# Diagonal chunk pairs computed on and above the diagonal only, the rest filled by TensorE transposes

## The chip, the cores and the metric

The kernel runs on one core of one Trainium2 chip. The metric is device time in microseconds (us) of that core. Before the change three runs took 1889.49, 1889.62 and 1890.78 us (median 1889.62); the profiled execution has a span of 1888.3 us and a mean granted TensorE clock of 0.987.

## The reference

```python
# layer 0, for each of 4 images; q is 4096 blocks-of-channel rows by 128 values here
energy = jnp.einsum('bci,bcj->bij', q, q)
d = jnp.sqrt(jnp.diagonal(energy, axis1=1, axis2=2))
energy = energy / (d[:, :, None] * d[:, None, :])
attn = jax.nn.softmax(energy, axis=-1)
out = jnp.einsum('bcj,bij->bci', q, attn)
out = gamma * out + xs
# layer 1, written short here; the reference spells it out; tokens of 128 channels
t = t + linear_attention(layernorm(t))      # 8 heads, no softmax
t = t + moe(layernorm(t))                   # router over 8 experts, top 2
```

The attention of layer 0 has 4096 positions with a vector of 128 values each. All vectors have length one once the energy is divided by `d`, so the scores are symmetric and at most 1, and no maximum is needed: `exp(energy)` is a symmetric 4096 by 4096 matrix, and its row sums divide the output at the end.

## The kernel before, in words

Everything is float32. For each image `b` (4 of them), `prep` loads four pieces `xx` of x, transposes them on TensorE to `qT` (positions on partitions), squares and reduces on VectorE (`sq`, `ss`), takes the inverse root on GpSimd (`rn`, line 109), scales (`qs`, line 190), and transposes back on TensorE (`ptn`, line 193) to `qn` (values on partitions, length one), which ScalarE copies out. A piece gives two chunks of 512 positions; there are 8 chunks (`NCH`) of 4 blocks (`NJ`) of 128.

`attend` walks over the pairs of chunks `(i, jc)` with `jc <= i`. A pair has four steps. In a step TensorE makes 128 by 512 scores (`pe`, line 242), ScalarE takes the exponential into `pr` with row sums (line 244), and TensorE multiplies by the values into the output bank `po` of chunk `i` (line 233), one step later than its scores. For `jc < i` the symmetric partner is needed too: VectorE transposes `pr` in 32 by 32 squares into `F` (line 248), 16 DMAs move the squares to their places in `G` (line 260, issued by SyncE), and later four matmuls of `G` (line 207, `transposed_share`) give chunk `jc` its part from chunk `i`, while ScalarE sums `G` (line 212) and VectorE adds the bank `pg` to the output `o` (line 218). Of `po` and `pg` there is one bank each, of `pe`, `pt` (all transposes and small products) and `py` two each. The pair on the diagonal, `jc == i`, is its own partner: its four steps compute all 512 by 512 scores, both halves of the symmetric square. It comes last in each `i`.

The transposed shares wait in the list `late`; one of their four steps is recorded in each step of `attend`, from `LAG` steps after the pair ended.

Layer 1 of image `b-1` (`layer1`, from line 273) is a generator of 151 small steps. While `attend(b)` runs, the main loop advances it, and the `prep` of image `b+1`, at set rates: a stream `(generator, begin, end, count)` takes `count` steps evenly between the steps `begin` and `end` of the 144. Layer 1 first divides the outputs by the row sums (`pbd`, `df`, line 342), adds them to the tokens on GpSimd (`T`, line 350), takes row statistics on VectorE (`bs_a` to `dm_a`, lines 311 to 320), the inverse root on GpSimd (`rsa`, line 109), `nba` on VectorE (line 322), normalises on ScalarE (`xn`, line 325) and forms the Gram matrix on TensorE (`pgram`, line 368). After that come attention rows, router and experts (`py`, lines 525 and 532). Layer 1 of the last image runs alone at the end.

The recording layer does not keep the written order as it stands: it plans each engine's order ahead of the run from the dependences, the buffers and estimates of its own, and the built program has one fixed list of instructions per engine. The engines meet at semaphores. The lists of the profiled execution are those of the built program, and they can be read for both kernels.

Of the kernel before, what the change touches and what calls it, by code (L numbers as in the profile page):

```python
# [1 line left out]

# [7 lines left out]
F32 = mybir.dt.float32  # L10
BF16 = mybir.dt.bfloat16
AF = mybir.ActivationFunctionType
# [6 lines left out]
def kernel(  # L19
# [10 lines left out]
    expert_b: bass.AP,  # L30
    out: bass.AP,
):

# [18 lines left out]
    nc = tc.nc  # L54
    P = 128
    B, C, H, W = x.shape
    N = (H // 2) * (W // 2)
    NB = N // P
    CH = 512
    NCH = N // CH  # L60
    NJ = CH // P
    HW2 = W // 2
    KT = 32
    S = 32
# [9 lines left out]
    ppool = ctx.enter_context(tc.tile_pool(name="ppool", bufs=6))  # L74
    fpool = ctx.enter_context(tc.tile_pool(name="fpool", bufs=2))
    gpool = ctx.enter_context(tc.tile_pool(name="gpool", bufs=3))
    work = ctx.enter_context(tc.tile_pool(name="work", bufs=2))
    stat = ctx.enter_context(tc.tile_pool(name="stat", bufs=2))
# [6 lines left out]
    def psum_t(name):  # L85
        return ps_t.tile([P, CH], F32, tag="pt", name=name)


    ident = const.tile([P, P], F32, tag="ident", name="ident")
# [60 lines left out]
    def load_tokens(dst, b, k0, nk):  # L150
        src = tokens(x, b)
        for s in range(2):
            for r1 in range(2):
                p0 = s * 64 + r1 * 32
                nc.sync.dma_start(dst[p0 : p0 + 32], src[s, r1, :, k0 : k0 + nk, :])
# [42 lines left out]

    late = []
    clock = [0]  # L200
    LAG = 4

    def transposed_share(b, st, i, jc, G):

        pg = ps_g.tile([P, CH], F32, tag="pg", name=f"pg_{b}_{i}_{jc}")
        for ib in range(NJ):
            nc.tensor.matmul(  # L207
                pg, st["qT"][i][:, ib, :], G[:, ib].rearrange("p a j -> p (a j)"),
                start=(ib == 0), stop=(ib == NJ - 1),
            )  # L210
            junk = work.tile([P, CH], BF16, tag="junk", name=f"junk_{b}_{i}_{jc}_{ib}")
            nc.scalar.activation(  # L212
                junk, G[:, ib].rearrange("p a j -> p (a j)"), AF.Copy,
                accum_out=st["sums"][:, NJ * i + ib, jc : jc + 1],
            )
            if ib == NJ - 1:
                o = st["o"][jc].rearrange("p (j a c) -> p a j c", a=4, c=S)
                nc.vector.tensor_tensor(o, o, pg.rearrange("p (a j c) -> p a j c", a=4, c=S), ALU.add)  # L218
            yield "done" if ib == NJ - 1 else None

    def attend(b, st):

        qT, qn = st.setdefault("qT", {}), st.setdefault("qn", {})
        st["sums"] = sums = stat.tile([P, NB, NCH], F32, tag="sums", name=f"sums_{b}")
        st["o"] = []

        for i in range(NCH):
            po = ps_o.tile([P, CH], F32, tag="po", name=f"po_{b}_{i}")
            pend = None

            def values(pend, i=i, po=po):
                pr, t = pend
                nc.tensor.matmul(po, qT[t // NJ][:, t % NJ, :], pr, start=(t == 0), stop=(t == NJ * (i + 1) - 1))  # L233

            for jc in range(i + 1):
                off = jc < i
                if off:
                    F = fpool.tile([P, CH // S, NJ, S], F32, tag="F", name=f"F_{b}_{i}_{jc}")
                for j in range(NJ):
                    t = NJ * jc + j  # L240
                    pe = ps_e.tile([P, CH], F32, tag="pe", name=f"pe_{b}_{i}_{t}")
                    nc.tensor.matmul(pe, qn[jc][:, ts(j, P)], qn[i], start=True, stop=True)  # L242
                    pr = ppool.tile([P, CH], F32, tag="pr", name=f"pr_{b}_{i}_{t}")
                    nc.scalar.activation(pr, pe, AF.Exp, accum_out=sums[:, t, i : i + 1])  # L244
                    if pend is not None:
                        values(pend)
                    if off:
                        nc.vector.transpose(F[:, :, j, :], pr)  # L248
                    pend = (pr, t)
                    clock[0] += 1  # L250
                    if late and late[0][0] <= clock[0]:
                        if next(late[0][1], "done") == "done":
                            late.pop(0)
                    yield
                if off:
                    G = gpool.tile([P, NJ, 4, P], F32, tag="G", name=f"G_{b}_{i}_{jc}")
                    blocks = F.rearrange("p (ib q) j c -> p q ib (j c)", q=4)
                    for a in range(4):
                        for q in range(4):
                            nc.sync.dma_start(G[ts(q, S), :, a, :], blocks[ts(a, S), q])  # L260
                    late.append((clock[0] + LAG, transposed_share(b, st, i, jc, G)))
            values(pend)
            o = opool.tile([P, CH], F32, tag="o", name=f"o_{b}_{i}")
            nc.vector.tensor_copy(o, po)
            st["o"].append(o)
# [7 lines left out]
    def layer1(b, st, alone):  # L273
# [5 lines left out]
        def psum_s(name):  # L279

            turn[0] += 1
            if alone and turn[0] % 4 == 1:
                return ps_o.tile([P, CH], F32, tag="po", name=name)
            if alone and turn[0] % 4 == 3:
                return ps_g.tile([P, CH], F32, tag="pg", name=name)
            return psum_t(name)
# [6 lines left out]

        load_tokens(T, b, 0, KT)
        yield
        den = stat.tile([P, NB], F32, tag="den", name=f"den_{b}")
        nc.vector.tensor_reduce(den, st["sums"], AX.X, ALU.add)
        rd = stat.tile([P, NB], F32, tag="rd", name=f"rd_{b}")
# [54 lines left out]
        def transpose_rows(g):  # L353
# [3 lines left out]
            if alone:  # L357
                if g % 4 == 0:
                    keep["G"] = gpool.tile([P, 4, 4, P], F32, tag="G", name=f"xnT_{b}_{g}")
                xnT = keep["G"][:, g % 4].rearrange("p j t -> p (j t)")  # L360
# [148 lines left out]
        for g in range(KT // 4):  # L509
            pt = psum_s(f"ptg_{b}_{g}")  # L510
# [8 lines left out]
            for jj in range(2):  # L519
                tmp = work.tile([P, 2, 4, D], F32, tag="wide", name=f"tmp_{b}_{g}_{jj}")  # L520
                for jk in range(2):
                    j = 2 * jj + jk
# [25 lines left out]
    states = [{} for _ in range(B)]  # L548
    STEPS = NJ * NCH * (NCH + 1) // 2
    LAST = STEPS - NJ * NCH  # L550
    SIDE = 152

    first = prep(0, 0, states[0])
    next(first)
# [4 lines left out]
    for b in range(B):  # L559
        streams = []  # L560
        if b == 0:
            for kc, begin, end in ((1, 0, 8), (2, 10, 26), (3, 30, 60)):
                streams.append((prep(0, kc, states[0]), begin, end, 9))
            streams.append((setup_weights(), 60, 70, 3))
        else:
            p = states[b - 1]
            work_left = layer1(b - 1, p, False)
            streams.append((work_left, 9, 138, SIDE))
        if b + 1 < B:
            for kc, at in enumerate((96, 121, 128, 134)):  # L570
                streams.append((prep(b + 1, kc, states[b + 1]), at, at + 9, 9))
        done = [0] * len(streams)
        for t, _ in enumerate(attend(b, states[b])):
            for n, (steps, begin, end, count) in enumerate(streams):
                while t >= begin and done[n] * (end - begin) < (t + 1 - begin) * count:
                    next(steps, None)
                    done[n] += 1
        for steps, *_ in streams:
            for _ in steps:
                pass  # L580
    finish_late()
    last = states[B - 1]
    for _ in layer1(B - 1, last, True):
        pass
# [38 lines left out]
```

## Time and profile before

| | before |
|---|---|
| median of 3 runs | 1889.62 us |
| span of the profiled execution | 1888.3 us |
| TensorE matmul busy | 1815.8 us, 96% of the span |
| ScalarE / VectorE / GpSimd busy | 51% / 48% / 15% |
| share of TensorE in the chain that ended last | 87% |
| `pe` matmuls (line 242), 512 columns | 1152 instructions, two to each product |
| `po` matmuls (line 233), 512 columns | 1152 |
| `pg` matmuls (line 207), 512 columns | 896 |

A float32 product shows as two matmul instructions. The mean duration of one (593 to 598 ns at 512 columns) is longer than the distance between two starts, because matmuls are pipelined: where TensorE is never short of work, a product of 512 columns starts every 0.858 us. What a matmul costs is read from that distance, in the timeline, and not from its duration. An idle time in front of an instruction has the releaser beside it: what the engine was waiting for.

### The profile page before, as it was taken

Reading aid. Unit: us, or ns where it says so; the run is one execution under the profiler, and the core shown is the slowest. Engines: PE = TensorE matmul, PEld = TensorE weight load, DVE = VectorE, ACT = ScalarE, POOL = GpSimd, SP = SyncE. Lnnn points to the kernel's source line nnn. Section 1 sums busy time; section 2 is a strip of 40 time slices with the busy share of each in tenths; the row PEclk is TensorE's granted clock in tenths of the full one; section 3 lists DMA queues with packets and bytes.
Section 4 is the critical chain, followed back from the end, with each engine's and each line's share of the span. In section 5 each row is a group of like instructions: output and inputs, shape, how many; then the busy total and the mean of one; then the engine's idle time right before and its main releaser. Section 6 shows DMA issues by size and latency. Waiting matters only on the chain.

```text
span 1888.3 us, 20141 instructions
## 1 busy us (share of the span) xinstructions
PE 1815.8 (96%) x5090; PEld 872.5 (46%) x5090; DVE 900.1 (48%) x2201; ACT 957.7 (51%) x2925; POOL 292.6 (15%) x275
## 2 busy tenths in 40 slices
PE   6999999999999999999999999999999999999588
PEld 3444444444554444444554444444455444444543
DVE  3343223345355454555455445563535544443676
ACT  2444444344556545554556545554545645544364
POOL 0000000003000121211200112221300022121336
PEclk9999999999999999999999999999999999999789
DMA  5333343431243233334233333333323323235001
GB/s 118 77 89 74 84 101 85 111 81 46 69 104 78 62 82 75 87 93 96 59 87 76 81 72 84 74 85 85 76 64 90 80 60 85 65 85 117 1 12 34
DMA packets 314274, 145.61 MB, mean 77 GB/s; under 512 B 32528, under 2 KB 314160, under 8 KB 314160
## 3 DMA queue, kind: packets, MB, share of 16 engines
q1 hardware_dynamic: 310528, 142.73, 32.4%
q10 hardware_dynamic: 3632, 1.60, 0.4%
q8 instruction: 42, 0.69, 0.2%
q14 instruction: 72, 0.59, 0.1%
HBM read 18.38 MB, written 8.39 MB: 14 GB/s over the span
## 4 chain that ended last, share of the span: by engine, by line
PE 87%; DVE 5%; POOL 3%; ACT 2%; SPq 1%; DMA 1%; issue 1%; ACTq 0%; POOLq 0%; DVEq 0%
PE po L233 24%; PE pe L242 24%; PE pg L207 20%; PE py L525 6%; PE py L532 5%; DVE df L342 1%; PE pbe L515 1%; PE pat L423 1%; SPq L260 1%; PE ptn L193 1%; POOL T L350 1%; ACT xn L325 1%; PE pgram L368 1%; POOL rsa L109 1%; PE ptx L356 1%; PE ptq L171 1%
## 5 line engine op out<-in xcount | busy, mean ns | idle before, releaser
L244 ACT ACTIVATE pr<-pe 128x512 f32<-128x512 f32 x576 | 343.9, 597 | 580.5 <-PE pe L242 580.1
L233 PE MATMUL po<-pr,qT 128*128 128x512 f32 x1152 | 590.3, 595 | 4.3 <-ACT pr L244 2.7
L248 DVE STREAM_TRANSPOSE F<-pr 128x512 f32<-128x512 f32 x448 | 311.4, 705 | 341.6 <-ACT pr L244 311.6
L242 PE MATMUL pe<-qn,qn 128*128 128x512 f32 x896 | 455.8, 593 | 0.2
L207 PE MATMUL pg<-G,qT 128*128 128x512 f32 x896 | 426.4, 598 | 2.8 <-DMA G<-F 2.8
L233 PEld LDWEIGHTS po<-pr,qT 128*128 128x128 f32 x1152 | 213.9, 190 | 272.1 <-issue 233.0
L212 ACT ACTIVATE junk<-G 128x512 bf16<-128x512 f32 x448 | 276.0, 623 | 4.9 <-DMA G<-F 4.9
L207 PEld LDWEIGHTS pg<-G,qT 128*128 128x128 f32 x896 | 171.0, 192 | 215.3 <-issue 209.3
L242 PEld LDWEIGHTS pe<-qn,qn 128*128 128x128 f32 x896 | 161.4, 190 | 161.1 <-issue 159.7
L534 ACT ACTIVATE tmp<-py,gate 128x128 f32<-128x128 f32 x512 | 145.7, 370 | 172.6 <-PE py L532 163.8
L527 DVE SCALAR_TENSOR_TENSOR acc<-py,gate,acc 128x128 f32<-128x128 f32 x512 | 174.9, 348 | 101.6 <-PE py L525 87.9
L218 DVE TENSOR_TENSOR o<-o,pg 128x512 f32<-128x512 f32 x112 | 76.8, 686 | 230.2 <-PE pg L207 228.9
L538 POOL TENSOR_TENSOR tmp<-tmp 128x512 f32<-128x512 f32 x64 | 81.3, 1271 | 559.2 <-ACT tmp L534 535.7
L532 PE MATMUL py<-ew_sb,xn 128*128 128x512 f32 x256 | 131.9, 601 | 4.1 <-ACT tmp L534 4.1
L242 PE MATMUL pe<-qn 128*128 128x512 f32 x256 | 131.0, 595 | 0.0
L525 PE MATMUL py<-ew_sb,xn 128*128 128x512 f32 x256 | 129.3, 592 | 0.0
L244 ACT ACTIVATION_READ_ACCUMULATOR pr<-pe 128x1 f32 x576 | 114.5, 199 | 0.0
L109 POOL TENSOR_TENSOR rn<-ss,neg_half 128x8 f32<-128x8 f32 x16 | 26.3, 1642 | 433.2 <-DVE ss L183 433.2
L212 ACT ACTIVATION_READ_ACCUMULATOR junk<-G 128x1 f32 x448 | 87.3, 195 | 0.0
L109 POOL TENSOR_TENSOR rsf<-dm_f,neg_half 128x8 f32<-128x8 f32 x16 | 26.3, 1644 | 359.2 <-DVE dm_f L320 359.2
L532 PEld LDWEIGHTS py<-ew_sb,xn 128*128 128x128 f32 x256 | 48.5, 192 | 65.1 <-issue 48.0
L525 PEld LDWEIGHTS py<-ew_sb,xn 128*128 128x128 f32 x256 | 48.0, 190 | 59.2 <-issue 39.4
(114 smaller groups left out, 1221.8 us busy)
## 6 DMA issues: line engine op xcount, KB each, us to landing
G<-F SPq DMA_DIRECT2D x1792, 64.0 KB, 2.0
xx<-in_x_dram SPq DMA_DIRECT2D x64, 128.0 KB, 3.0
T<-in_x_dram SPq DMA_DIRECT2D x16, 512.0 KB, 5.7
out_dram<-acc SPq DMA_DIRECT2D x128, 64.0 KB, 1.8
ew_sb<-in_L_ffn_expert_w_dram ACTq DMA_DIRECT2D x1, 512.0 KB, 5.5
raw_w<-in_L_attn_Wv_dram ACTq DMA_DIRECT2D x1, 512.0 KB
raw_w<-in_L_attn_Wk_dram ACTq DMA_DIRECT2D x1, 256.0 KB
raw_w<-in_L_attn_Wq_dram ACTq DMA_DIRECT2D x1, 256.0 KB
```

The source lines that it names most:

```text
L207: nc.tensor.matmul(pg, st["qT"][i][:, ib, :], G[:, ib].rearrange("p a j -> p (a j)"), start=(ib == 0), stop=(ib == NJ - 1),)
L212: nc.scalar.activation(junk, G[:, ib].rearrange("p a j -> p (a j)"), AF.Copy, accum_out=st["sums"][:, NJ * i + ib, jc : jc + 1],)
L218: nc.vector.tensor_tensor(o, o, pg.rearrange("p (a j c) -> p a j c", a=4, c=S), ALU.add)
L233: nc.tensor.matmul(po, qT[t // NJ][:, t % NJ, :], pr, start=(t == 0), stop=(t == NJ * (i + 1) - 1))
L242: nc.tensor.matmul(pe, qn[jc][:, ts(j, P)], qn[i], start=True, stop=True)
L244: nc.scalar.activation(pr, pe, AF.Exp, accum_out=sums[:, t, i : i + 1])
L248: nc.vector.transpose(F[:, :, j, :], pr)
L525: nc.tensor.matmul(py, xn[:, k, :], ew_sb[:, 0:4, :], start=True, stop=True)
L527: nc.vector.scalar_tensor_tensor(acc[:, j, :], py[:, ts(e, D)], gate[:, k, e : e + 1], acc[:, j, :], ALU.mult, ALU.add)
L532: nc.tensor.matmul(py, xn[:, k, :], ew_sb[:, 4:8, :], start=True, stop=True)
L534: nc.scalar.activation(tmp[:, jk, e, :], py[:, ts(e, D)], AF.Copy, scale=gate[:, k, 4 + e : 5 + e])
L538: nc.gpsimd.tensor_tensor(tmp[:, :, 0:2], tmp[:, :, 0:2], tmp[:, :, 2:4], ALU.add)
```

## The change

On the diagonal pair a step `j` now computes the scores only from its own block on: 512, 384, 256 and 128 columns instead of four times 512. The blocks below the diagonal are the transposes of those above. TensorE transposes them (6 transposes of 128 by 128 for each chunk, into a `pt` bank), ScalarE copies them out with row sums (into a further column of `sums`), and three narrower matmuls (128, 256, 384 columns) add them to the same `po` bank. The two buffers for it come from the ring of 6 that `pr` uses.

With it go some moves:

- the diagonal pair comes first in each `i` and not last, but for the last `i` of the last image, where it stays last;
- the extra matmuls are held back until the third step of the next pair (`given`), where there is one;
- `clock` counts TensorE work in units of 128 columns instead of steps, a late step counts too, and `LAG` is 56 of these;
- `F` and `G` are laid out so that a row that a DMA moves is 2 KB in one piece, and not four of 512 B;
- layer 1 of the image before begins at step 14 and not 9, with 166 steps up to step 140 and not 152 up to 138; three of the four `prep` streams start 3 steps later (124, 131, 137).

The purpose is to take matmul columns off TensorE, and to keep the late matmuls at a fixed distance in TensorE time.

```diff
-    LAG = 4
+    LAG = 56
...
-        st["sums"] = sums = stat.tile([P, NB, NCH], F32, tag="sums", name=f"sums_{b}")
+        st["sums"] = sums = stat.tile([P, NB, NCH + 1], F32, tag="sums", name=f"sums_{b}")
+        nc.gpsimd.memset(sums[:, :, NCH:], 0.0)
...
+            ending = b == B - 1 and i == NCH - 1
+            order = list(range(i)) + [i] if ending else [i] + list(range(i))
...
+            def below(tiles, blks, i=i, given=given):
+                pt = psum_t(f"ptd_{b}_{i}_{blks[0]}")
+                gd = ppool.tile([P, CH], F32, tag="pr", name=f"gd_{b}_{i}_{blks[0]}")
+                at = 0
+                for ib in blks:
+                    for j in range(ib):
+                        nc.tensor.transpose(pt[:, at + P * j : at + P * j + P], tiles[j][:, ts(ib, P)], ident)
+                    w = gd[:, at : at + P * ib]
+                    nc.scalar.activation(
+                        w, pt[:, at : at + P * ib], AF.Copy, accum_out=sums[:, NJ * i + ib, NCH:]
+                    )
+                    given.append(partial(values, w, NJ * i + ib, 0, P * ib))
+                    at += P * ib
...
+                    c0 = 0 if jc < i else P * j
-                    nc.tensor.matmul(pe, qn[jc][:, ts(j, P)], qn[i], start=True, stop=True)
+                    nc.tensor.matmul(pe[:, c0:], qn[jc][:, ts(j, P)], qn[i][:, c0:], start=True, stop=True)
-                    nc.scalar.activation(pr, pe, AF.Exp, accum_out=sums[:, t, i : i + 1])
+                    nc.scalar.activation(pr[:, c0:], pe[:, c0:], AF.Exp, accum_out=sums[:, t, i : i + 1])
+                    flush()
+                    if j == 1:
+                        pend.extend(given)
+                        given.clear()
+                    pend.append(partial(values, pr[:, c0:], t, c0, CH))
...
+                    if jc == i and j in (1, 2):
+                        pend.append(partial(below, own, (2, 1) if j == 1 else (3,)))
+                    clock[0] += 2 * (CH - c0) // P
                     if late and late[0][0] <= clock[0]:
+                        clock[0] += NJ
...
-                            nc.sync.dma_start(G[ts(q, S), :, a, :], blocks[ts(a, S), q])
+                            nc.sync.dma_start(
+                                G[ts(q, S), a].rearrange("p ib f -> p (ib f)"),
+                                F[ts(a, S), q].rearrange("p ib j c -> p (ib j c)"),
+                            )
...
-    SIDE = 152
+    SIDE = 166
+    BEGIN = 14
...
-            streams.append((work_left, 9, 138, SIDE))
+            streams.append((work_left, BEGIN, 140, SIDE))
-            for kc, at in enumerate((96, 121, 128, 134)):
+            for kc, at in enumerate((96, 124, 131, 137)):
```

## The prediction, on record before the changed kernel ran

> **What bounds the kernel now.** I read the busy shares first, then the chain that ended last, then what TensorE waits for.
>
> ```profile
> PE 1815.8 (96%) x5090; PEld 872.5 (46%) x5090; DVE 900.1 (48%) x2201; ACT 957.7 (51%) x2925; POOL 292.6 (15%) x275
> ...
> PE 87%; DVE 5%; POOL 3%; ACT 2%; SPq 1%; DMA 1%; issue 1%; ACTq 0%; POOLq 0%; DVEq 0%
> ```
>
> TensorE is busy for 96% and makes up 87% of the chain; the others are half idle. So matmul time removed anywhere between start and end is time gained, unless TensorE then waits. What it waits for between 50 us and the end of the last attention (1725 us) is little:
>
> ```profile
> PE ptn L193 <- DVE qs L190: 6.6, 4, 3.0
> PE pgram L368 <- ACT xn L325: 5.1, 4, 2.8
> PE po L233 <- ACT pr L244: 2.7, 2, 1.4
> ```
>
> These are all side work: `prep` of the next image, and layer 1 of the image before. The timeline shows how one comes about:
>
> ```profile
> 347.80 1.11 PE L171 MATMUL ptq<-ident,xx 128*128 128x128 f32 x8
> ...
> 348.74 1.02 PE L233 MATMUL po<-pr,qT 128*128 128x512 f32 x2
> 349.60 1.02 PE L242 MATMUL pe<-qn,qn 128*128 128x512 f32 x2
> ...
> 352.79 1.64 POOL L109 TENSOR_TENSOR rn<-ss,neg_half 128x8 f32<-128x8 f32 x1 [64.08 <-DVE ss L183]
> 354.46 1.29 DVE L190 TENSOR_TENSOR qs<-qT,rn 128x512 f32<-128x512 f32 x2 [1.81 <-POOL rn L109]
> 355.29 1.69 PE L193 MATMUL ptn<-ident,qs 128*128 128x128 f32 x8 [2.96 <-DVE qs L190]
> ...
> 356.78 4.79 PE L207 MATMUL pg<-G,qT 128*128 128x512 f32 x8
> ```
>
> From the end of the `ptq` transposes (348.74) VectorE and GpSimd need 6.55 us until `ptn` can start. TensorE executes its fixed list: it had six products between, at 0.858 us each (349.60 - 348.74), 5.15 us at warm clock and before semaphores, and stood still for the rest. So a chain's wait is its length less the matmul work that the list puts inside it. Afterwards the `pg` group takes 4.6 us to the next start (361.41) instead of 4 x 0.858 = 3.43: the clock had fallen (granted 0.86 over 352 to 364 us). The same shape in layer 1, and at the end:
>
> ```profile
> 899.87 3.19 ACT L325 ACTIVATE xn<-T,nba,rsa 128x128 f32<-128x128 f32 x8 [2.98 <-DVE nba L322]
> ...
> 917.27 1.12 PE L233 MATMUL po<-pr,qT 128*128 128x512 f32 x2 [1.36 <-ACT pr L244]
> ```
>
> ```profile
> 1738.34 5.27 PE L207 MATMUL pg<-G,qT 128*128 128x512 f32 x8 [2.78 <-DMA G<-F]
> ```
>
> Eight normalises hold ScalarE for 3.2 us, and an exponential queued behind them holds `po`. The last `pg` waits 2.78 us for its DMA and then runs 1.7 us slow.
>
> [...] four `ptn` that start at 818.86 us are followed by the next product at 819.29, so one takes 0.109 us from TensorE.
>
> **The change, part by part.** There are 32 chunks (4 images, 8 each).
>
> *Removed*: 768 of 2048 score columns on each diagonal: 768/512 x 0.858 = 1.287 us. The `po` products keep 2048 columns (1280 above, 768 below): nothing.
> *Added*: six transposes, 6 x 0.109 = 0.65 us, and a few ns for narrower instructions (128-column Gram products come every 0.111 us, not 0.107), 0.05 us.
> Sum: -0.58 us x 32 = **-18.5 us** of TensorE work. All of it lies on the bound.
>
> *ScalarE* loses 768 exponential columns and gets three copies with their accumulator reads a chunk: about +1.1 us x 32 = 35 us on an engine 51% busy. Hidden by the matmuls of the next pair, since `given` is held back; not where there is no next pair before it (first chunk of each image). *VectorE*, the wider DMA rows, `LAG`: no matmul waits for a `G` before 1725 us, so nothing. *Tail*: with the longer lag one more group of four `pg` (3.43 us) is left for the time of the last DMA. That fills the wait of 2.78 us and keeps the clock: -4.5 us; less 1.1 us for the single `pg` bank (VectorE's addition between two groups back to back): **-3.4 us**.
>
> *The new order.* I went through TensorE's list in the built program, with 0.858 us for 512 columns and 0.109 for a transpose. For the kernel before this reproduces its waits: the list puts 5.15, 3.43, 5.15 and 5.15 us inside the four `prep` chains of the first image, so waits of 1.4, 3.1, 1.4 and 1.4; the trace has 1.4, 3.0, 1.0 and 1.2. For images 2 and 3 it puts 8.6 to 14.6 us there, and there is no wait. After the change the fourth `prep` runs over the end of its image, and the first chunk of the next image has only narrow products to offer. The list puts `ptq`, `ptn` directly behind each other in the first image (0 us inside), and 2.6 us inside in the second and third:
>
> - waits 6.55, 3.95, 3.95 us, where before 1.24, 0, 0. Nothing can pass `ptn`: behind it stand the transposes `ptd` of the first chunk, which need the two `pt` banks that `ptn` fills and ScalarE empties (0.6 us each), then copies (about 0.4, 0.3 and 0.5 us, between 597 ns at 512 columns and 308 at 128), then the held products. At the fallen clock I count 5.9 us from the first `ptn` to the end of these for 3.0 us of work: 2.9 us more each time. The bounds: 1.0 if the clock stays[...]. Sum: (6.55 + 2.9 - 1.24) + 2 x (3.95 + 2.9) = **+21.9 us**.
> - Layer 1 beside chunks 2 and 3. Before, the run loses 8.0, 4.6 and 4.6 us there against the count of its list. After, ScalarE's list in images 3 and 4 has 16 normalises in one piece, then four sums of `G` and two copies, and only then the exponential of the first full pair of chunk 3. VectorE reaches the statistics only after the transposes of chunk 2: nine instructions from the first `bn_stats` to the first `xn` take 9.2 us (890.69 to 899.87), the second eight start about 4.9 us later, end 3.2 us later, and 3.5 us of sums, copies and the exponential follow. The `po` behind it stands at 41.5 us in the list's count and can go at 48.8 (50.6 at low clock): 8.2 us lost instead of 4.6. Image 2 comes out at 8.6 against 8.0. Sum: 0.6 + 2 x 3.6 = **+7.8 us**; bounds 0 and 14, since such a chain through four engines is easily 2 us off.
> - Head and single-bank waits at the first chunks: +1. Denser side work (1.32 steps of layer 1 to a step instead of 1.18): +1, from 0 to 4; the kernel before lost 1.4 us in a whole image outside its Gram part.
>
> Total: -18.5 - 3.4 + 21.9 + 7.8 + 2 = **+9.8 us**, so 1899.4 us.
>
> **Rivals.**
> - *Faster: the matmul work decides.* For it: 87% of the chain is TensorE, and the chains could fit in if VectorE runs ahead. Against: the lists are fixed. With waits as before: 1889.6 - 18.5 - 3.4 = 1867.7; with half of the new losses (21.9 + 7.8 + 2 = 31.7) 1883.6.
> - *No change*: the stalls at the three image ends cost only their idle time (6.55 + 2 x 3.95 - 1.24 = 13.2), with no fallen clock, and layer 1 half of what I count: -21.9 + 13.2 + 3.9 + 2 = -2.8, so 1886.8. For it: only one of the waits is longer than the 3 us after which a fallen clock was seen. Against: the stalls of `ptn` and `ptd` follow closely on each other.
> - *Transposes and narrow products cost their full duration* (0.288 instead of 0.109 us; loading weights, 190 ns each, becomes the bound): 192 x 0.18 + 576 instructions x 0.08 = 80 us more at worst; a fifth of it gives 1915. Against it: warm groups of transposes and Gram products run at 0.109 and 0.111 us.
>
> **How the numbers follow.** Slower as forecast 0.54; full durations 0.06; no change 0.17; faster 0.23. The range takes in no change and most of the dearer end, and leaves out the clean gain: 1876 to 1912. Over 0.2% is 3.8 us: slower 0.60, within 0.17, faster 0.23.
>
> **What would show it.** TensorE's `pe` work down by 25% of its diagonal part and 192 transposes at starts 0.11 us apart; TensorE idle before `ptn`, `ptd` and the held `po` up to about 7 to 10 us at each of three image ends, with the granted clock down for a few us; `po` waiting for ScalarE some 7 us in the Gram part of images 3 and 4; no wait for the last `G`. Wrong if those places are free of waits, or if the wide DMA rows or the layout of `G` change the speed of `pg` (0.858 us) itself.

## The result, and the profile after

The changed kernel takes 1913.9 us (median of four runs, 1912.5 to 1917.7), against 1889.9 before: a ratio of 1.0129, interval 1.0112 to 1.0147. It is slower, as forecast, but by 24.0 us and not by 9.8, and just outside the range (1876 to 1912).

The busy shares and the chain of the changed kernel:

```profile
PE 1817.3 (95%) x5474; PEld 921.4 (48%) x5474; DVE 907.9 (47%) x2201; ACT 974.8 (51%) x3117; POOL 293.1 (15%) x279
...
PE 79%; DVE 8%; SPq 4%; POOL 4%; ACT 2%; DMA 2%; issue 1%; ACTq 0%; DVEq 0%; POOLq 0%
```

Two things are to be seen. TensorE's busy time went up by 1.5 us although its list has 18.5 us less work: busy time counts durations, which overlap, and which were longer where the granted clock was low (eight `ptn` take 1.94 us at the end of image 2, shown below, with a granted clock of 0.61 over 858 to 866 us, against 1.23 in e11), so it can't be read as work. And its share of the chain fell from 87% to 79%: VectorE, GpSimd and SyncE took its place, which means that TensorE now waits for chains through them. What it waits for between 50 and 1750 us:

```profile
PE ptn L195 <- DVE qs L192: 19.3, 6, 6.4
PE po L240 <- ACT pr L274: 7.6, 6, 2.6
PE pg L209 <- DVE o L219: 6.6, 5, 1.9
PE pgram L409 <- ACT xn L366: 4.2, 2, 2.1
PE ptf L483 <- ACT xg L366: 1.5, 3, 0.5
PE ptd L251 <- ACT gd L253: 1.1, 2, 0.6
```

`ptn` went from 6.6 to 19.3 us, as forecast. `po` went from 2.7 to 7.6 us, but not where it was forecast. The prediction put this wait into the Gram part beside images 3 and 4. These are the waits around the Gram part beside image 2 (430 to 500 us), and then beside image 3 (880 to 935 us); beside image 4 they are the same as beside image 3:

```profile
PE po L240 <- ACT pr L274: 6.9, 5, 2.6
```

```profile
PE pgram L409 <- ACT xn L366: 2.1, 1, 2.1
PE ptd L251 <- ACT gd L253: 0.6, 1, 0.6
```

New, and not forecast, are `pg` waiting for VectorE to add the share before it to `o` (6.6 us, five times), and `ptf`, a transpose of layer 1, waiting for ScalarE (three times).

**A balance.** Waits alone leave out what the low clock takes afterwards (0.61 over those 8 us, behind a wait of 3.73 us). So I went through the timeline of TensorE, took for each row the distance to the next start, and subtracted what its instructions cost where the granted clock is 1.00 (0.429 us for an instruction of 512 columns, in proportion below that and 3 ns more, 0.109 for a transpose). What is left is *lost time*. From the first product to the last the work so counted is 1770.3 us before and 1754.1 after, the lost time 98.8 and 142.6; -16.2 + 43.8 = 27.6, which is the difference of the two spans (1915.9 - 1888.3). This count has a grain: a row of the timeline shows the shape of its first instruction only, so rows that mix widths are priced wrong, mostly too high, in the changed kernel. Priced instruction by instruction, the work differs by -18.5 us, as in the lists, and the lost time by +46.1 (99.3 and 145.4). The table is by rows; a single place moves by about 1 us at most (after: the first 330 us to 20.6, the ends of images 2 and 3 to 14.9). The profiled run after is the longest of the four, so 3.6 us of this are not in the medians. By place, in us, with the runs below that matter most:

| lost time of TensorE | before | after | forecast of the difference | difference | e3 | e4 | e6 | e11 |
|---|---|---|---|---|---|---|---|---|
| first 330 us | 19.2 | 19.5 | +1 | +0.3 | 19.7 | 19.7 | 20.1 | 20.0 |
| end of image 1 | 8.8 | 15.4 | +8.2 | +6.6 | 15.0 | 16.2 | 13.1 | 13.1 |
| ends of images 2, 3 | 1.3 | 15.8 | +13.7 | +14.5 | 4.9 | 4.5 | 4.3 | 4.7 |
| Gram part, layer 1 of image 1 | 8.4 | 10.3 | +0.6 | +1.9 | 5.1 | 6.6 | 10.2 | 4.9 |
| Gram part, images 2, 3 | 8.9 | 15.9 | +7.2 | +7.0 | 17.0 | 13.2 | 15.6 | 17.2 |
| late groups ahead of the ends of images 2, 3 | 0.3 | 8.0 | } +1 | +7.7 | 2.4 | 0.6 | 4.6 | 6.3 |
| the rest of the images | 2.7 | 9.5 | } | +6.8 | 6.5 | 5.0 | 8.2 | 5.6 |
| from 1690 us | 49.2 | 48.1 | -3.4 | -1.1 | 47.9 | 50.3 | 47.2 | 45.3 |

(e3: preps at the times of before; e4: layer 1 at the times of before; e6: chains filled; e11: chunk 0 full. Gram part of image 1 means its layer 1, which runs beside image 2; those of images 2 and 3 run beside images 3 and 4.)

**An image end.** TensorE at the end of image 2 in the changed kernel:

```profile
850.60 1.11 PE L173 MATMUL ptq<-ident,xx 128*128 128x128 f32 x8
851.54 0.60 PE L272 MATMUL pe<-qn 128*128 128x256 f32 x2
851.98 0.81 PE L240 MATMUL po<-pr,qT 128*128 128x384 f32 x2
852.62 0.38 PE L272 MATMUL pe<-qn 128*128 128x128 f32 x2
852.85 0.60 PE L240 MATMUL po<-pr,qT 128*128 128x256 f32 x2
853.28 1.02 PE L272 MATMUL pe<-qn 128*128 128x512 f32 x2
858.03 1.94 PE L195 MATMUL ptn<-ident,qs 128*128 128x128 f32 x8 [3.73 <-DVE qs L192]
859.81 0.69 PE L251 MATMUL ptd<-ident,pr 128*128 128x128 f32 x2
860.66 1.11 PE L251 MATMUL ptd<-ident,pr 128*128 128x128 f32 x4 [0.17 <-ACT qn L197]
861.57 0.63 PE L240 MATMUL po<-pr,qT 128*128 128x128 f32 x2
```

The chain from `ptq` to `ptn` (851.54 to 858.03) is 6.5 us long, and only four narrow products and a full one, 2.6 us, stand inside. Behind the wait the granted clock is 0.61 over 858 to 866 us: eight `ptn` take 1.78 us to the next start instead of 0.87, six `ptd` 1.76 instead of 0.65. The narrow products ahead of the wait cost what their columns say: 256 columns 0.44 us to the next start (851.54 to 851.98), 384 columns 0.64, 128 columns 0.23.

**A late group.** Some 50 us ahead of that, in the same kernel:

```profile
798.80 1.65 POOL L111 TENSOR_TENSOR rn<-ss,neg_half 128x8 f32<-128x8 f32 x1 [7.12 <-DVE ss L185]
...
800.48 1.75 DVE L192 TENSOR_TENSOR qs<-qT,rn 128x512 f32<-128x512 f32 x1 [1.50 <-POOL rn L111]
800.48 1.02 PE L209 MATMUL pg<-G,qT 128*128 128x512 f32 x2
...
803.55 0.69 DVE L281 STREAM_TRANSPOSE F<-pr 128x512 f32<-128x512 f32 x1
804.17 0.30 DVE L568 SCALAR_TENSOR_TENSOR acc<-py,gate,acc 128x128 f32<-128x128 f32 x1
804.41 0.66 DVE L219 TENSOR_TENSOR o<-o,pg 128x512 f32<-128x512 f32 x1
...
805.12 1.12 PE L209 MATMUL pg<-G,qT 128*128 128x512 f32 x2 [1.91 <-DVE o L219]
```

The last product of one share starts at 800.48. The first of the next, two products later in the list, needs the one `pg` bank. That product is done at 801.50, and VectorE could empty the bank from there. But it has stood 1.5 us for GpSimd's inverse root of a `prep`, and in its own order two `qs`, three `acc` and an `F` come first (not all of them shown); the sum starts at 804.41. In the rest of the images two smaller losses stand three times each: a late group that waits 0.9 us (1.1 us lost each time), and `ptf`, which waits 0.5 us for ScalarE's `xg` in layer 1 (1.2 us lost each time).

**The tail.** The last two late groups of the changed kernel (the second waited 2.78 us for its DMA before):

```profile
1760.05 3.60 PE L209 MATMUL pg<-G,qT 128*128 128x512 f32 x8
...
1764.43 3.70 PE L209 MATMUL pg<-G,qT 128*128 128x512 f32 x8 [0.78 <-DVE o L219]
```

The DMA is no longer waited for, as forecast; the single bank costs 0.95 us there (1764.43 - 1760.05 - 3.43). From 1690 us to the start of the first `pbd` (at 1743.45 and 1767.97 us) the lost time, priced instruction by instruction, is 4.8 us before and 1.3 after, so 3.5 us less; but the layer 1 that follows loses 47.6 us instead of 44.6.

### The profile page after: what moved, and what is told of

Same layout as the page of the kernel before. It is cut to its first block, busy times and chain, and to the rows that moved or that the text cites. A ratio compares the mean times of both kernels' runs of the same rounds, so it can differ in the third digit from the quotient of the medians.

```text
span 1915.9 us, 21142 instructions
## 1 busy us (share of the span) xinstructions
PE 1817.3 (95%) x5474; PEld 921.4 (48%) x5474; DVE 907.9 (47%) x2201; ACT 974.8 (51%) x3117; POOL 293.1 (15%) x279
## 4 chain that ended last, share of the span: by engine, by line
PE 79%; DVE 8%; SPq 4%; POOL 4%; ACT 2%; DMA 2%; issue 1%; ACTq 0%; DVEq 0%; POOLq 0%
PE po L240 22%; PE pe L272 19%; PE pg L209 17%; PE py L573 5%; PE py L566 5%; SPq L295 4%; PE pat L464 1%; PE pbe L556 1%; DVE F L281 1%; DVE df L383 1%; POOL rsa L111 1%; PE ptd L251 1%; PE ptn L195 1%; DVE bs_a L352 1%; PE pgram L409 1%
## 5 line engine op out<-in xcount | busy, mean ns | idle before, releaser
L274 ACT ACTIVATE pr<-pe 128x512 f32<-128x512 f32 (+1 forms) x576 | 323.7, 562 | 526.7 <-PE pe L272 523.3
L240 PE MATMUL po<-pr,qT 128*128 128x512 f32 (+3 forms) x1152 | 551.9, 561 | 9.3 <-ACT pr L274 7.6
L209 PE MATMUL pg<-G,qT 128*128 128x512 f32 x896 | 443.8, 597 | 7.6 <-DVE o L219 7.4
L272 PEld LDWEIGHTS pe<-qn,qn 128*128 128x128 f32 x896 | 159.2, 191 | 145.5 <-issue 145.4
L579 POOL TENSOR_TENSOR tmp<-tmp 128x512 f32<-128x512 f32 x64 | 81.4, 1272 | 511.4 <-ACT tmp L575 511.3
L272 PE MATMUL pe<-qn 128*128 128x512 f32 (+3 forms) x256 | 90.1, 442 | 0.0
```

Source lines behind the costliest of these rows:

```text
L209: nc.tensor.matmul(pg.rearrange("p (a f) -> p a f", a=4), st["qT"][i][:, ib, :], G[:, :, ib], start=(ib == 0), stop=(ib == NJ - 1),)
L240: nc.tensor.matmul(po[:, lo:hi], qT[blk // NJ][:, blk % NJ, :], w, start=(count[0] == 1), stop=(count[0] == total))
L272: nc.tensor.matmul(pe[:, c0:], qn[jc][:, ts(j, P)], qn[i][:, c0:], start=True, stop=True)
L274: nc.scalar.activation(pr[:, c0:], pe[:, c0:], AF.Exp, accum_out=sums[:, t, i : i + 1])
L579: nc.gpsimd.tensor_tensor(tmp[:, :, 0:2], tmp[:, :, 0:2], tmp[:, :, 2:4], ALU.add)
```

## The experiments

Theory going in: the moves put `prep` and layer 1 where TensorE has too little work to hide them, at the ends and the Gram part, and the rest of the loss comes from the late groups in front of the single bank. Rivals: the triangle itself costs more than counted (narrow products, transposes, ScalarE's copies), or the moves lose by themselves. Medians of the kernel before, beside these runs, are 1889.5 to 1890.8.

**e1, the triangle alone**, and **e2, the moves alone.** e1 is the changed kernel with all moves undone:

```diff
-            ending = b == B - 1 and i == NCH - 1
+            ending = True
...
-                    clock[0] += 2 * (CH - c0) // P
+                    clock[0] += 1
...
-            for kc, at in enumerate((96, 124, 131, 137)):
+            for kc, at in enumerate((96, 121, 128, 134)):
```

(and `LAG`, `SIDE`, `BEGIN` and the layout of `F` and `G` as before). e2 keeps the moves and computes full diagonal pairs:

```diff
-                    c0 = 0 if jc < i else P * j
+                    c0 = 0
```

> The kernel before with the triangle alone: the diagonal pair stays last in each chunk, and the lag, the layout of F and G, and the times of prep and layer 1 are those of before. If it was the moves that lost the time: -18.5 us of TensorE work; the list puts 2.2, 3.4, 2.2 and 0.9 us inside the four prep chains of the first image (waits 4.4, 3.1, 4.4 and 5.7 instead of 1.4, 3.1, 1.4 and 1.4: +10.3 us), and 8.6 us or more in images 2 and 3 (none), so about 1882 us. If narrow products and transposes cost more than 0.109 us each for 128 columns, or ScalarE's copies hold the products: 1900 us or more. If the head, ends and layer 1 are as before and the first image gets by: 1872.

> The changed kernel with all its moves, but the diagonal pairs compute all their columns (no transposes, no held products). Its list has 18.5 us more TensorE work, 5.1 us inside each fourth prep chain (waits of 1.4 instead of 6.5, 4.0 and 4.0 us). If the moves lose time only where the narrow first chunk leaves nothing inside the chain: about 1913.9 + 18.5 - 20 = 1912, still slower than before because of layer 1's place and the sums behind the one bank of the late shares. If the moves alone are harmless: 1890. If they alone carry the whole loss: 1913.9 + 18.5 = 1932.

e1 took 1904.7 us (ratio 1.0072, 1.0055 to 1.0089), e2 1894.3 (1.0017, 1.0010 to 1.0023). With 1890.8 before and 1913.9 after, this is a square of four: the moves add 3.5 us to full pairs and 9.2 to the triangle, the triangle adds 13.9 us without the moves and 19.6 with them, although it takes 18.5 us of work away. My theory blamed the moves for too much. e1's waits:

```profile
PE ptn L195 <- DVE qs L192: 16.9, 4, 5.5
PE po L240 <- DVE o L300: 9.7, 3, 4.7
PE pgram L405 <- ACT xn L362: 7.0, 3, 3.1
```

Its four chains in the first image wait 4.2, 3.0, 4.2 and 5.5 us, close to the 4.4, 3.1, 4.4 and 5.7 of the list. Its `pe` instructions of 128, 256 and 384 columns start every 0.112, 0.216 and 0.323 us in their median, its `ptd` every 0.109 us (in the changed kernel, above, a product of two such instructions takes 0.23, 0.44 and 0.64 us), so narrow products and transposes do cost what was counted. By the balance it loses 9.6 us more than before in the first 330 us, 10.4 at the end of the first image and 4.2 in the Gram part after it, and another 6.8 in the Gram parts of images 2 and 3; in the middle and at the ends of images 2 and 3 it loses no more than 0.4 us more. In the first 330 us it is the first of those chains, with its wait of 4.2 us and what is lost behind it; in the Gram parts `po` waits for VectorE, which copies the one `po` bank out behind the work of layer 1 (9.7 us). So the rival "the triangle costs more than counted" is wrong as to TensorE's work. At the end of the first image the triangle takes away the work that hid the chains of `prep`, as the list had it. Why the Gram parts lose more with it is not shown.

**e3, the preps at the times of before**, **e4, layer 1 at the times of before**, and **e5, both**, each in the changed kernel:

```diff
-            for kc, at in enumerate((96, 124, 131, 137)):
+            for kc, at in enumerate((96, 121, 128, 134)):
```

```diff
-    SIDE = 166
-    BEGIN = 14
+    SIDE = 152
+    BEGIN = 9
...
-            streams.append((work_left, BEGIN, 140, SIDE))
+            streams.append((work_left, BEGIN, 138, SIDE))
```

> The changed kernel with the prep streams at the times of before (121, 128, 134 instead of 124, 131, 137). The list then puts 4.5, 6.0 and 6.0 us inside the three fourth chains (waits 2.0, 0.5 and 0.5 instead of 6.5, 4.0 and 4.0) and no two late groups two products apart at the end of images 2 and 3. If prep running over the image's end is the main loss: 4.5 + 7 less idle, some 6 us less at a low clock and 7 us less in front of the late groups: about 1890. If the ends are held by the buffers that the diagonal pair in front keeps longer (the buffer that qT needs is not free before the second pair of the last chunk is done), the waits move to the copies of ptq: 1905 to 1920.

> The changed kernel with layer 1 at the times of before (from step 9 to 138, 152 steps). The list puts 6.0 us instead of 2.6 inside the fourth chain of images 2 and 3 (waits 0.5 instead of 4.0), the first image stays (6.5), and the late groups two products apart at 465, 903 and 1340 us of work are gone. If the denser layer 1 is the second cause: 7 us of idle, 6 us of low clock and 3 us in front of late groups less, about 1898. If layer 1's place has nothing to do with it: 1912 to 1916.

> The changed kernel with both the prep streams and layer 1 at the times of before; triangle, diagonal pair in front, lag and layout stay. Its list puts 15 us inside the fourth chains of images 2 and 3 and no two late groups two products apart before the last chunk; in the first image 4.3, 3.4 and 4.5 us inside (waits 2.3, 3.1 and 2.0). If the loss is where work stands at the image ends and in front of the late groups: about 1885 (e4's 1891.9 less some 7 us, mostly at the end of the first image and of image 3), faster than before. If the triangle loses elsewhere too: 1890 or more.

e3 took 1895.1 us (1.0022, 1.0014 to 1.0031), e4 1891.9 (1.0004, 0.9996 to 1.0013), e5 1897.6 (1.0045, 1.0030 to 1.0060). The first two took 19 and 22 us off the changed kernel, e4 more than I expected. Both brought the ends of images 2 and 3 from 15.8 to 4.9 and 4.5 us, each because its list has 6.0 us inside the fourth chain. In e4 the waits of `pg` are gone as well:

```profile
PE ptn L195 <- DVE qs L192: 14.5, 6, 6.4
PE pgram L409 <- ACT xn L366: 3.9, 2, 2.0
PE po L240 <- DVE o L304: 3.5, 3, 1.8
```

Late groups two products apart are still in its list; but VectorE isn't held at that moment (8.0 us lost in the changed kernel, 0.6 here). The changed kernel itself has a sixth such place, at 1724.8 us, and `pg` does not wait there. So the distance of two products was not the cause alone: it takes a VectorE that is late in its own order. e5 missed its forecast of 1885: at the end of the first image it loses 18.7 us, more than e3 and e4, where three chains wait 2.1, 3.0 and 2.1 us and the `ptn` behind each are slow (eight take 1.14, 1.74 and 1.32 us to the next start instead of 0.87); and the Gram part after it loses some 5 us more than in e4. The two cures do not add.

**e6, the chains filled.** Work that nobody needs, inside the three chains:

```diff
+        if kc == 3 and b > 0:
+            fill = psum_t(f"fill_{b}")
+            for n in range(4):
+                nc.tensor.matmul(fill, ident, ew_sb[:, 0:4, :].rearrange("p e d -> p (e d)"), start=(n == 0), stop=(n == 4 - 1))
```

> The changed kernel with four products of 512 columns of constants more inside each of the three fourth prep chains; nothing reads them (3.43 us each, 10.3 us of work added). The list then has 3.4, 4.7 and 4.7 us inside the chains instead of 0, 2.6 and 2.6: 7.6 us less waiting. If the some 3.5 us that each end loses after its wait are TensorE's low clock, they shrink to 1 us: -7.5 + 10.3 - 7.6 = -5, about 1909. If they are the waits for the transposes' banks and ScalarE: +2.7, about 1917.

1907.2 us (1.0091 of before): 6.7 us less than the changed kernel, with 10.3 us more TensorE work. The stretches around the end of image 2, first the changed kernel, then e6; the columns are the length, the busy time of TensorE matmuls, of weight loads, VectorE, ScalarE and GpSimd, and then the granted clock, the DMA share and GB/s:

```profile
854.00:858.00 4.00, 0.30 (x1) 0.00 (x0) 2.19 (x5) 0.00 (x0) 1.63 (x1) 0.92 0.41 99
858.00:866.00 8.00, 7.80 (x31) 5.93 (x31) 1.18 (x2) 4.18 (x16) 0.00 (x0) 0.61 0.36 82
866.00:874.00 8.00, 8.00 (x26) 4.19 (x26) 1.00 (x2) 4.84 (x20) 0.00 (x0) 1.00 0.00 1
```

```profile
850.00:854.00 4.00, 3.79 (x11) 1.71 (x9) 2.56 (x4) 0.00 (x0) 1.26 (x1) 1.00 0.44 107
854.00:862.00 8.00, 6.75 (x33) 4.77 (x34) 1.98 (x3) 4.67 (x17) 0.38 (x1) 1.00 0.42 99
862.00:870.00 8.00, 8.00 (x28) 4.12 (x27) 1.40 (x2) 5.02 (x20) 0.00 (x0) 1.00 0.00 1
```

In the changed kernel the clock is 0.61 over the 8 us behind the wait; in e6 it stays at 1.00, and the wait is 1.45 us. Between 840 and 880 us e6 loses 2.1 us. The waits for the transposes' banks behind `ptn`, which I had counted as their own cost (0.17 us of waiting in the changed kernel), go with the low clock: in e6 no `ptd` waits there. At the end of image 1 the wait fell from 6.39 to 2.39 us only, and what stands behind it is still slow: eight `ptn` take 1.48 us to the next start instead of 0.87, six `ptd` 1.80 instead of 0.65.

**e11, chunk 0 full.** The changed kernel, with full columns in the first diagonal pair of each image:

```diff
-                    c0 = 0 if jc < i else P * j
+                    c0 = 0 if jc < i or i == 0 else P * j
```

> The changed kernel, but the diagonal pair of chunk 0 of each image computes all its columns (no transposes there): 4 x 0.58 = 2.3 us more TensorE work. The list now finds 3.5, 5.1 and 5.1 us for the inside of the three fourth prep chains instead of 0, 2.6 and 2.6. If the narrow first chunk is what leaves those chains empty: 8.6 us less waiting, and no waits for transposes' banks and less low clock behind it (5 us), so 1913.9 + 2.3 - 8.6 - 5 = 1903. If other work of the ends decides: 1914 to 1916.

1893.8 us (1.0020, 1.0012 to 1.0028). This gives 2.3 us of work back and gains 20, twice what was forecast. The end of image 2 in it:

```profile
839.87 1.11 PE L173 MATMUL ptq<-ident,xx 128*128 128x128 f32 x8
840.82 1.02 PE L240 MATMUL po<-pr,qT 128*128 128x512 f32 x2
841.67 1.02 PE L272 MATMUL pe<-qn 128*128 128x512 f32 x2
842.53 1.02 PE L240 MATMUL po<-pr,qT 128*128 128x512 f32 x2
843.39 1.02 PE L272 MATMUL pe<-qn 128*128 128x512 f32 x2
844.25 2.07 PE L240 MATMUL po<-pr,qT 128*128 128x512 f32 x4
847.30 1.23 PE L195 MATMUL ptn<-ident,qs 128*128 128x128 f32 x8 [0.99 <-DVE qs L192]
848.37 1.67 PE L272 MATMUL pe<-qn 128*128 128x512 f32 x4
```

Full products fill the chain, `ptn` waits 1 us, and what follows is little slowed (eight `ptn` take 1.07 us to the next start instead of 0.87, the two products behind them 1.80 instead of 1.72). Of the 25.4 us of lost time that are gone, 13.4 are at the three ends, as expected; the others are in the Gram part of image 1 (5.4), the middle (3.9), the tail (2.8) and the late groups (1.7). None of these was touched by the edit itself: they moved with the planned order.

**e7, the first image's chains spread**, and **e9** and **e10**, on top of e5's times:

```diff
+            first = ((96, 105), (112, 126), (121, 137), (133, 144))
+            rest = ((96, 105), (121, 130), (128, 137), (134, 143))
+            for kc, (at, end) in enumerate(first if b == 0 else rest):
+                streams.append((prep(b + 1, kc, states[b + 1]), at, end, 9))
```

In e9 GpSimd issues the loads of the two last pieces of image 2, and e10 has the later times for images 3 and 4 on top of that:

```diff
-        load_tokens(xx.rearrange("p k w r -> p k (w r)"), b, 8 * kc, 8)
+        load_tokens(xx.rearrange("p k w r -> p k (w r)"), b, 8 * kc, 8, nc.gpsimd if b == 1 and kc > 1 else None)
...
-            rest = ((96, 105), (121, 130), (128, 137), (134, 143))
+            rest = ((96, 105), (124, 133), (131, 140), (137, 146))
```

> As the run with both old times, and in the first image, which has no layer 1 beside it, the preps of the next image start earlier and last longer (from step 112, 121 and 133, over 14, 16 and 11 steps). The list has 19 us inside each of these three chains. If their waits and low clock cost the 8 us that the end of the first image still loses: some 8 us below that run, about 1877. If the copies of ptq then hold VectorE until the last pairs set the buffers of qT free, waits appear at po for ScalarE or VectorE in that stretch: no gain, or up to 10 us slower than that run.

> As the run with the preps of the first image spread, and the loads of the two last pieces of the second image's x are issued by GpSimd, so that SyncE's queue with the DMAs of G doesn't stand behind a load that waits for a buffer. That run lost 10.8 us more than the kernel before ahead of 330 us, nearly all at a late group that waited 6.1 us for its DMA and at the low clock after it. If the queue is the whole cause: 10 us less, 1892.1 - 10 = 1882, faster than before. If GpSimd, standing at the load, then delays an inverse root: a wait of a few us at ptn in its place, 1886 or more.

> As the run before it, but the preps of images 3 and 4 start at 124, 131 and 137 as in the changed kernel (layer 1 stays at the times of before). The list leaves 6.0 us inside the fourth chains there (waits of 0.5 us) and two late groups two products apart once in each image. If the waits for VectorE's sum come back with that: 3 to 8 us more than the run before it. If it is not the distance of the groups, but VectorE's own queue at that moment, that counts (the run with only layer 1's times of before had that distance and no such wait): within 2 us of it.

They took 1892.1, 1891.4 and 1892.4 us (ratios 1.0012, 1.0006 and 1.0008; that of e9 reaches from 0.9997 to 1.0015): e7 missed its forecast of 1877 and e9 its 1882. The end of the first image fell from 18.7 to 8.2 us, what the kernel before loses, but a late group now waits for its DMA. First e7, then e9:

```profile
PE pg L209 <- DMA G<-F: 6.1, 1, 6.1
```

```profile
PE pg L209 <- DMA G<-F: 6.2, 1, 6.2
```

My explanation after e7, that loads in SyncE's queue held up the DMAs of `G`, fell with e9: without them the wait is the same. SyncE itself waits there for VectorE's `F` (in e9 25.4 us in three waits between 225 and 345 us), and in the list three late groups follow with 1.3 us of other work between the first two and none before the third, which comes earlier than its data. e10 kept the two-product distance and had no wait of `pg` for VectorE (late groups lose 0.7 us), as its second theory said.

**e8, two banks for `pg`**, one for `py`:

```diff
-    ps_g = ctx.enter_context(tc.tile_pool(name="ps_g", bufs=1, space=PSUM))
+    ps_g = ctx.enter_context(tc.tile_pool(name="ps_g", bufs=2, space=PSUM))
...
-    ps_y = ctx.enter_context(tc.tile_pool(name="ps_y", bufs=2, space=PSUM))
+    ps_y = ctx.enter_context(tc.tile_pool(name="ps_y", bufs=1, space=PSUM))
```

> The changed kernel with two banks for the late shares (pg) and one instead of two for the experts' products (py). If the waits of pg for VectorE's sum cost 6.6 us of idle and some 4 us of low clock behind it, these vanish: -10 us, so about 1904 less what the single py bank costs (between 512 tiles it may wait for ScalarE or VectorE each time; 0 to 30 us, to be read at py). If the waits of pg only stand in for another wait: no change where they were.

1967.4 us (1.0411). The time lost in front of `pg` fell from 12.3 to 1.9 us, so its waits were the bank's; in front of `py` it rose from 7.4 to 55.5, more than I had allowed for, most of it in the last image's layer 1, which runs alone.

```profile
PE py L566 <- DVE acc L568: 21.7, 12, 2.2
...
PE py L573 <- ACT tmp L575: 8.7, 12, 1.2
```

In both lines the next products wait until VectorE or ScalarE has read the one `py` bank: a wait moved, and grew.

**e12 to e15, versions put together** from these: in e12 the first image as before and chunk 0 full in the others; in e13 chunk 0 full with layer 1 at e4's times; in e14 the same with layer 1 from step 11 to 140; in e15 with e5's times. The lines of e12 for the triangle, and of e14 for layer 1:

```diff
-                    c0 = 0 if jc < i else P * j
+                    c0 = P * j if jc == i and (b > 0 and i > 0) else 0
...
-    SIDE = 166
-    BEGIN = 14
+    SIDE = 152
+    BEGIN = 11
```

> A version made from what the runs showed: the first image stays as in the kernel before (all columns, diagonal pair last, prep at 121, 128 and 134), images 2 to 4 have the triangle in front except in chunk 0, prep at 124, 131 and 137 in images 3 and 4, layer 1 at the times of before. TensorE's list is 1771.6 - 1759.4 = 12.2 us shorter. If the first image then loses what it loses in the kernel before, and the rest some 9 us more than there, as in the run with layer 1 at the old times: 1890.4 - 12.2 + 9 = 1887, a little faster than before. If the ends move with the rest: 1890 to 1893.

> The changed kernel with chunk 0 full and layer 1 at the times of before. Each alone took some 20 us off the changed kernel (to 1893.8 and 1891.9). They share the ends of images 2 and 3, some 12 us together; what is left to each alone is the waits at the end of the first image (chunk 0) and those for VectorE's sum and at the Gram matrix (layer 1). If the two causes are separate where they don't overlap: 1893.8 less 4 us in front of late groups, less 4 to 8 us at the Gram matrix: 1883 to 1887, faster than before. If the ends were the only cause and the rest is chance of the planned order: 1890 to 1894.

> As the run before it, with layer 1 from step 11 to 140 in 152 steps, so between the two. If the losses at the Gram matrix follow the exact place of layer 1's steps: anywhere between 1885 and 1896. If the density of layer 1's steps (1.18 to a step of attend) is what counts: within 2 us of the run before it.

> Chunk 0 full, layer 1 and the preps at the times of before. Without the full chunk 0 the same times gave 1897.6, with 18.7 us lost at the end of the first image. The list leaves 6.0 us instead of 4.5 inside its fourth chain (wait 0.5), and 15 us in images 3 and 4. If the narrow chunk 0 was the loss: some 5 us less, 1893. If the first image's end loses to its other two chains (waits of 2.3 and 3.1 us): within 2 us of 1897.6 + 2.3.

They took 1897.5, 1894.3, 1906.9 and 1896.5 us (1.0039, 1.0022, 1.0087 and 1.0035). e12 and e14 lie outside both of their forecasts, e15 between its two, and e13 at the edge of the second. In e13 the ends of images 2 and 3 lose 4.4 us, as with either cure alone, and the first image's end and its Gram part 27.1 where e11 has 18.0. So the cures share the ends; the rest that each seemed to bring did not add up. e14 has the density of e13 (1.18 steps of layer 1 to a step) and lost 12.6 us to it: `po` waits for ScalarE 14.5 us in eleven places, against 2.1 in three.

```profile
PE po L240 <- ACT pr L274: 14.5, 11, 3.5
```

At equal density a shift of layer 1 by two steps costs this much, so the density alone does not decide. No version beat the kernel before; e4 and e9 come level with it.

## Why the prediction was wrong

- *Removed and added work*, -18.5: right. The trace's instructions priced one by one give -18.5, and the distances of narrow products and transposes, in the changed kernel and in e1, bear out the prices. A `pg` product still starts every 0.858 us, so the new layout of `G` did not slow it. With these prices the rival of full durations falls, though its 1915 lay nearest to the result.
- *The image ends*, +21.9: right in place and size, +21.1 by rows (6.6 and 14.5), 20.6 by instructions. The waits were 6.4, 3.7 and 3.7 us for a forecast of 6.55, 3.95 and 3.95. e3, e6 and e11 each gave the ends of images 2 and 3 more work inside the chain, and each took about 11 us off there. One line was misread: between `ptq` and the `ptn` at 355.29 us stand four products, 3.43 us, and not six; with four, the chain of 6.55 us gives the wait of 3.1 us that the prediction's own list has for it (2.96 in the trace). What I put down to `pt` banks and ScalarE behind the wait was mostly the clock (over the 8 us behind the wait 0.61 in the changed kernel and 1.00 in e6).
- *Layer 1's Gram part*, +7.8: +8.9 (1.9 and 7.0). The size is right, but by luck: the wait is another one. Forecast was `po` behind an exponential that stands after 16 normalises, beside images 3 and 4. There `po` does not wait at all; `pgram` itself waits 2.1 us for the first of the normalises, which come late, and `ptd` 0.6 us, with a granted clock of 0.83 over 918 to 928 us. The `po` that waits for ScalarE is beside image 2 (6.9 us), where hardly any loss was forecast. And the two places of images 2 and 3 lost from 13.2 to 17.2 us in the runs of the table.
- *The tail*, -3.4: -1.1. Up to the first `pbd` it is -3.5: the wait for the DMA went, as forecast, and the single bank cost 0.95 us. But some 3 us more were lost in layer 1 behind it; why is not shown.
- *"Denser side work ...: +1, from 0 to 4"*, and with it "*VectorE*, the wider DMA rows, `LAG`: ... nothing": **this is the step that failed.** The balance puts 14.5 us there: 7.7 in the late groups ahead of two image ends, 6.8 over the rest of the images. Some 11 us of it are late groups in front of the single `pg` bank, 3.7 us are `ptf` behind ScalarE's `xg`. I wrote that no matmul waits for a `G`, which holds, but let it stand for the late groups as a whole: the single bank was counted in the tail, and with at most 1 us at the head and the first chunks. The list of the changed kernel has five places ahead of the tail where the next late group comes two products after the last; that of the kernel before has none. Each needs VectorE's sum in between, and `pg` waited for it 0.9 us in three of them and 1.9 in two, with a granted clock of 0.72 after these two (806 to 812 and 1266 to 1272 us). I had looked at chains of `prep` and layer 1 in TensorE's list, not at VectorE's order between two uses of one bank. With two banks (e8) these waits are gone. Nor does density explain it: e4 and e14 have the same density, and lose 5.6 and 14.2 us in these two rows.

Of the 17.8 us that the profiled runs differ more than forecast, 13.5 are this term, 2.3 the tail, and 2.3 lie in the rows' pricing of the work; the others nearly cancel. The range's end, 1912, is about what the sum gives with every bound at its dear end (6.2 for the Gram part, 3 for denser side work, and 3.3 for the ends, which was my estimate of a longer low clock and rests on no trace); the term that failed took 14.5 against a bound of 4.

What stays open: why an edit at chunk 0 moves 5 us in a Gram part 50 us later, or a shift of layer 1 by two steps 12 us. The planned order changes with each edit, and no run isolates its choices. Nor were the new layout of `F` and `G`, the longer `LAG` or the diagonal pair in front tried each by itself: e1 and e2 take all moves together. And what brings the loss in the Gram part is read from waits alone.

## What to carry to other kernels

Work taken off a busy engine is a gain only where nothing was hidden behind it (here 18.5 us of work went and 46 us of lost time came): before cutting, list what chains through other engines run inside the instructions that go, and look first at the seams (the first unit of a loop, the end of an image), where e11 gained 20 us by *giving back* 2.3 us of work. For each buffer with one copy, read the emptying engine's own order between two uses, not only the distance of the uses. In a kernel at 95% of its bound, count the waits with the low clock behind them (here a wait of 3.73 us cost about 7.5), and expect the side work's exact place to be worth as much as the change.

## What the runs showed of the hardware

- Two waits of 3.73 us of TensorE cost about 7.5 us each in all: the granted clock was 0.61 and 0.57 over the 8 us behind them (858 to 866 and 1318 to 1326 us). 10.3 us of useless products inside three waits (6.39, 3.73 and 3.73 us) made the kernel 6.7 us faster (e6).
- Shorter waits were followed by a lower clock too: 2.96 us in the kernel before by 0.74 over 356 to 362 us. The length alone does not decide: 1.91 us in front of a late group at 805.12 us was followed by 0.72 over 806 to 812 us; in e11 two groups waited 1.91 us as well, and in one place (796.73 us) the next three products started 0.85 to 0.86 us apart, in the other (1250.41 us) the group's own product and the next took 1.63 and 1.70 us to the next start.
- Busy time of TensorE rose by 1.5 us while its work fell by 18.5 us.
- A product of 128, 256 and 384 columns takes 0.23, 0.44 and 0.64 us to the next start, 512 columns 0.86: in proportion to the columns, while the weight loads of `pe` beside them last 191 to 194 ns each on average. A 128 by 128 transpose takes 0.109 us.
